# A sparse four-layer graph network on one core: the second half's tail is advanced ahead of the first, and query and input steps are emitted ahead of tail steps

## The chip, the cores and the metric

The kernel runs on one core of a Trainium2 chip. The core has five engines that run side by side, each through its own stream of instructions in the order in which they were emitted: PE (matrix multiplication, with its weight loads shown apart as PEld), DVE (elementwise work and reductions), ACT (activations and copies out of PSUM), POOL (here: the issue of gathers, and small elementwise operations) and SP (issue of plain DMAs). The metric is the time of the device in microseconds (us), lower is better.

## What is computed

The input `x` holds 16 graphs' features, 16 x 1024 x 128 in float32, and `adj` one 1024 x 1024 adjacency matrix with about 8 edges a row that all graphs share. Four layers follow one another. Layers 0, 2 and 3 are attention over the neighbours with a feed-forward block:

```python
Q, K, V = h @ Wq, h @ Wk, h @ Wv                    # 8 heads of 16
scores = where(adj == 0, -inf, Q K^T / 4)
x = h + (softmax(scores) V) @ Wo + bo
x = layer_norm(x)                                   # gain, shift
x = layer_norm(x + relu(x @ W1 + b1) @ W2 + b2)
```

Layer 1 is a graph attention with one head, whose scores are leaky sums of two terms per edge, followed by a residual and one layer norm; it has no feed-forward block.

## The kernel before

**Units and parts.** Since the graph is sparse, keys and values of every node lie in a DRAM table, and the kernel gathers the rows of each node's neighbours. Work is cut into units: layer, group of eight graphs (two groups), tile of 128 nodes (eight tiles), 64 units in all. A unit's edges are cut into parts. In an attention layer tile 0 has seven parts and every other tile five; the last part of a unit ("MIX") is half as large as the others. Part by part, DVE multiplies gathered keys by the queries (`products`, L868), reduces to scores (`exponentials`, L891), ACT takes the exponential (L895), DVE multiplies gathered values by it (`weighted`, L919), and PE sums the products by node (`summed`, L935, tile `acc`). POOL issues the gathers for the part four ahead (`gathered`, L856).

**Tails.** When a unit's sums are done, `divided` has DVE divide them, in two halves of four graphs each, into two tiles `o`, and starts one tail for each half. A tail is a Python generator: each `yield` ends a step. The steps of `attention_tail` are, in order:

- s0: PE transposes `o` (L596), ACT copies the result (`oT`, L598) and adds the bias to `x` (L640)
- s1: PE multiplies by `Wo` and by `centre` (L644, L645)
- s2: ACT squares with a running sum (L580); s3: POOL raises to the power -1/2 (L586); s4: ACT scales (`z`, L589)
- s5: PE transposes `z` (L596), ACT writes `x1` (L600)
- s6: PE multiplies by `W1` (L655), ACT takes the relu (`f1`, L659)
- s7: PE multiplies by `W2` and `centre` (L664, L668)
- s8, s9, s10: squares, power and scale again
- s11: PE transposes `z`, ACT writes `xT`; s12 and s13: PE multiplies by the next layer's `Wkv` (L538), ACT copies (L542); s14: SP writes the table. In the last layer s12 is a second transpose and copy (`outs`), and s13 POOL's scattered write of the output (L625).

The second half's tail begins with one empty step, so it is one step behind. `advance` gives every tail in the list one step.

**What sets the order.** The order is written out by hand: the main loop over parts emits, for each part, products, the sums of two parts before, `others()`, exponentials, `others()`, the weighted products of the part before and a gather, `others()`. I call these three calls slots 1, 2 and 3 of a part. Each call advances the tails at a pace that spreads 16 steps over a unit (about one per slot), and then takes one step of something else: `queries` of the next unit, or else `loaded` (in layer 0, the input of the unit after next), or else a step that projects the other group's input (`slow`, layer 0's first group only). Counting the five-part unit's parts from zero, the queries' four steps come in slots 2 and 3 of part 1 and slots 1 and 2 of part 2: PE multiplies by `Wq` (L819) and ACT copies `q` (L823), then four matmuls spread the rows over partitions (L828) into four PSUM tiles and ACT copies them into `qr` (L831); then the same for the second half. The tails of the unit before take their steps from slot 3 of part 1 on:

| slot | first half | second half | other step |
|---|---|---|---|
| part 1, 3 | s0 | (empty) | queries: spread, first half |
| part 2, 1 | s1 | s0 | queries: Wq, second half |
| part 2, 2 | s2 | s1 | queries: spread, second half |
| part 2, 3 | s3 | s2 | (queries end) |
| part 3, 1 | s4 | s3 | layer 0: POOL issues the gather of the first half's `rows` (L784) |
| part 3, 2 | s5 | s4 | |
| part 3, 3 | s6 | s5 | layer 0: PE transposes `rows`, ACT copies; POOL issues the second half's |
| part 4, 1 | s7 | s6 | |
| part 4, 2 | s8 | s7 | layer 0: the second half's `rows` are transposed |
| part 4, 3 | s9 | s8 | |
| next unit, part 0, slots 1, 2, 3 | s10, s11, s12 | s9, s10, s11 | |
| next unit, part 1, slot 1 | s13 | s12 | |
| next unit, part 1, slot 2 (two steps of the tails) | s14 | s13, s14 | queries: Wq, first half |

**Buffers.** `bank` hands out PSUM tiles from a pool of four; a transpose, a `W1` product or one spread matmul takes one of them each, and it is free again when ACT has copied it. The tails' sums have two PSUM tiles of their own (`yps`). `f1` is single, `oT`/`x1` and `z` are double.

Of the kernel before, what the change touches and what calls it, by code (L numbers as in the profile page):

```python
# [12 lines left out]
F32 = mybir.dt.float32  # L13
# [7 lines left out]
P = 128  # L21
D = 128
H = 8
HD = 16
FF = 256
F = FF // P
# [17 lines left out]
G = B // GR  # L44
HF = 2
GH = G // HF
# [4 lines left out]
J = P // 32  # L51
# [37 lines left out]
MOST = max(sum(map(len, _pieces)) for _pieces in PIECES)  # L89
# [33 lines left out]
def sparse_path(ctx: ExitStack, tc: tile.TileContext, a: dict, out: bass.AP, flag):  # L123
# [9 lines left out]
    def bank(shape):  # L133
        return banks.tile(shape, F32, tag="ps", name="ps")
# [39 lines left out]
    reps = ctx.enter_context(tc.tile_pool(name="reps", bufs=2))  # L174
    ones_ = ctx.enter_context(tc.tile_pool(name="ones_", bufs=1))
    twos = ctx.enter_context(tc.tile_pool(name="twos", bufs=2))
    exps = ctx.enter_context(tc.tile_pool(name="exps", bufs=2))
    scratch = ctx.enter_context(ExitStack())
    s1 = scratch.enter_context(tc.tile_pool(name="s1", bufs=1))
# [425 lines left out]
    def finish(l, g, t, h, z, gain, shift):  # L605
# [22 lines left out]
            in_=o.rearrange("p g d -> p (g d)"), in_offset=None,  # L628
        )

    def attention_tail(l, g, t, h, o):
        layer = LAYERS[l][0]
        p = {n: w[layer, n] for n in ATTN if (layer, n) in w}
        xt = xs[l, g, t][:, h]
        for _ in range(h):
            yield
        oT = twos.tile([P, GH, P], F32, tag="oT", name="oT")
        turned(o, oT)

        nc.scalar.activation(xt, xt, AF.Identity, bias=p["bo"])  # L640
        yield
        ps = ybanks.tile([P, GH, D], F32, tag="yps", name="yps")
        for i in range(GH):
            nc.tensor.matmul(ps[:, i, :], oT[:, i, :], p["Wo"], start=True, stop=False)  # L644
            nc.tensor.matmul(ps[:, i, :], xt[:, i, :], centre, start=False, stop=True)  # L645
        yield
        z = yield from normed(ps)
        yield
        x1 = twos.tile([P, GH, P], F32, tag="oT", name="x1")
        turned(z, x1, p["ln1_g"], p["ln1_b"])  # L650
        yield
        f1 = ones_.tile([P, F, GH * P], F32, tag="f1", name="f1")
        for f in range(F):
            ps = bank([P, GH * P])
            nc.tensor.matmul(  # L655
                ps, p["W1"][:, f * P : (f + 1) * P], x1.rearrange("p g n -> p (g n)"),
                start=True, stop=True,
            )
            nc.scalar.activation(f1[:, f, :], ps, AF.Relu, bias=p["b1"][:, f : f + 1])  # L659
        yield  # L660
        ps = ybanks.tile([P, GH, D], F32, tag="yps", name="yps")
        for i in range(GH):
            for f in range(F):
                nc.tensor.matmul(  # L664
                    ps[:, i, :], f1[:, f, i * P : (i + 1) * P], p["W2"][:, f, :],
                    start=(f == 0), stop=False,
                )
            nc.tensor.matmul(ps[:, i, :], x1[:, i, :], centre, start=False, stop=True)  # L668
        yield
        z = yield from normed(ps)  # L670
        yield
        yield from finish(l, g, t, h, z, p["ln2_g"], p["ln2_b"])
# [55 lines left out]
    def at_once(g):  # L728

        spare = reps.tile([P, J, ROW], F32, tag="qr", name="spare")  # L730

        def fetch(t):
            if t < T:
                nc.sync.dma_start(
                    spare[:, t % J, :], a["x"][t * P : (t + 1) * P, columns(g, 0, HF)]
                )

        for t in range(3):
            fetch(t)
        yield  # L740
        for t in range(T):
            fetch(t + 3)
            rows = spare[:, t % J, :].rearrange("p (h g d) -> p h g d", h=HF, g=GH)
            both = []
            for h in range(HF):
                kv = None
                if h:
                    kv = exponents()[:, : 2 * GH * D].rearrange("p (c g d) -> p c g d", c=2, g=GH)
                both.append(natural(g, t, h, rows[:, h], kv))
            while both:  # L750
                advance(both)
                yield

    def exponents():
        return exps.tile([P, max(MOST, 2 * D // HD) * G * H], F32, tag="ex", name="ex")


    units = [(l, g, t) for l in range(len(LAYERS)) for g in range(GR) for t in range(T)]
# [8 lines left out]
    es, prs, exs, qs, qx, ofs, accums = {}, {}, {}, {}, {}, {}, {}  # L767

    def is_attention(u):
        return LAYERS[units[u][0]][1] is ATTN  # L770
# [28 lines left out]
    def queries(u):  # L799

        l, g, t = units[u]
        if not is_attention(u):
            ps = bank([P, J + 1, G])
            for j in range(J):
                nc.tensor.matmul(ps[:, j, :], rep_of(j, True), srcs[g, t], start=True, stop=True)
            for k, j in enumerate(SHARED[t]):
                at = slice(64 * k, 64 * k + 64)
                nc.tensor.matmul(
                    ps[at, MIX, :], rep_of(j, True)[:, at], srcs[g, t], start=True, stop=True
                )  # L810
            ofs[u] = smalls.tile([P, J + 1, G], F32, tag="of", name="of")
            nc.scalar.copy(ofs[u], ps)
            return
        qs[u] = reps.tile([P, J, ROW], F32, tag="qr", name="qr")
        for h in range(HF):
            q = ones_.tile([P, GH * D], F32, tag="q", name="q")
            ps = bank([P, GH, D])
            for i in range(GH):
                nc.tensor.matmul(  # L819
                    ps[:, i, :], xs[l, g, t][:, h, i, :], w[LAYERS[l][0], "Wq"],  # L820
                    start=True, stop=True,
                )
            nc.scalar.copy(q, ps.rearrange("p g d -> p (g d)"))  # L823
            yield
            pss = []
            for j in range(J):
                ps = bank([P, GH * D])
                nc.tensor.matmul(ps, rep_of(j), q[32 * j : 32 * j + 32], start=True, stop=True)  # L828
                pss.append(ps)
            for j in range(J):  # L830
                nc.scalar.copy(qs[u][:, j, h * GH * D : (h + 1) * GH * D], pss[j])  # L831
            yield
# [49 lines left out]
    def exponentials(i):  # L882
        u, pieces = parts[i]
        t = units[u][2]
        heads = H if is_attention(u) else 1
        sc = smalls.tile([P, es[i].shape[1], G * heads], F32, tag="sc", name="sc")
        if u not in exs:
            exs[u] = exponents()[:, : MOST * G * heads].rearrange("p (c a) -> p c a", a=G * heads)
        ex, n = exs_of(i)
        if is_attention(u):  # L890
            nc.vector.tensor_reduce(  # L891
                sc[:, :n, :], prs[i][0][:, :n, :].rearrange("p k (a d) -> p k a d", d=HD),
                mybir.AxisListType.X, ALU.add,
            )
            nc.scalar.activation(ex, sc[:, :n, :], AF.Exp, scale=1.0 / HD**0.5)  # L895
        else:
            k = 0
            for piece in pieces:
                m = k + len(piece)
                nc.vector.tensor_tensor(  # L900
                    sc[:, k:m, :], es[i][:, k:m, ROW:], of_piece(ofs[u], piece), ALU.add
                )
                k = m
            nc.vector.scalar_tensor_tensor(
                sc[:, :n, :], sc[:, :n, :], SLOPE, sc[:, :n, :], ALU.mult, ALU.max
            )
            nc.scalar.activation(ex, sc[:, :n, :], AF.Exp)
# [55 lines left out]
    def divided(u):  # L963

        l, g, t = units[u]
        heads, d = (H, HD) if is_attention(u) else (1, D)
        den = bank([P, G * heads])
        for n, c in enumerate(sum(PIECES[t], [])):
            marked(t, c, den, exs[u][:, n, :])
        both = smalls.tile([P, 2, G * heads], F32, tag="both", name="both")  # L970
        yield
        nc.vector.reciprocal(both[:, 1, :], den)
        for h in range(HF):
# [14 lines left out]
    tails = []  # L988
# [2 lines left out]
    slow = []  # L991

    def advance(gens):
        for gen in list(gens):
            if next(gen, "end") == "end":
                gens.remove(gen)

    pace = [0.0, 0.0]

    def idle():  # L1000
        return slow if held[0] or not busy[0] else []

    def others():
        pace[0] += pace[1]
        while pace[0] >= 1.0:
            advance(tails)
            pace[0] -= 1.0
        for gens in (fronts or loads or idle(),):
            if not gens:
                continue  # L1010
            got = next(gens[0], "end")
            if got == "end":
                gens.pop(0)
            if got == "idle":
                advance(idle())

    with tc.manual_schedule():
        wide = [gather_buffer() for _ in range(EDGES)]
# [27 lines left out]
        smalls = ctx.enter_context(tc.tile_pool(name="smalls", bufs=3))  # L1046
# [8 lines left out]
        for i in range(len(parts) + 2):  # L1055
            here = i < len(parts)
            u = parts[i][0] if here else len(units)
# [58 lines left out]
            advance(tails)  # L1116


    fine = smalls.tile([P, 2, G * H], F32, tag="both", name="fine")
    nc.vector.tensor_scalar(fine, seen, LIMIT, None, ALU.is_lt)  # L1120
    counts = const.tile([P, 3], F32, name="counts")
    nc.vector.tensor_reduce(counts[:, 0:1], fine, mybir.AxisListType.XY, ALU.min)
# [428 lines left out]
```

## Time and profile before

| | |
|---|---|
| three runs | 2548.26, 2549.46 and 2554.35 us, median 2549.46 |
| the profiled execution's own time | 2562.74 us |
| span in its profile | 2561.0 us, mean granted PE clock 0.911 |
| busy, share of the span | PE 82%, DVE 75%, ACT 58%, POOL 57%, PEld 51% |
| DMA | 636 MB, 248 GB/s over the span |

How to read it: each engine's busy time is its instructions' own; a wait is idle time of an engine ahead of an instruction, put down to what ended it. PE's matmuls are pipelined and their ends modelled. In a line of the timeline the columns are start and length in us, the engine, the line of the kernel, the operation, output and input by name, the shapes, how many instructions were merged, and in brackets the idle time before and what released it. The stages, read from which lines run: up to about 200 us the graph is sorted and the first table is built; layer 0 runs until about 860 us, layer 1 until about 1200, layer 2 until about 1890, layer 3 to the end. A unit of an attention layer takes some 38 to 42 us, a unit of layer 1 some 20.

### The profile page before, as it was taken

What the parts mean: (1) busy time and instruction counts of PE and PEld (TensorE: products, weight loads), DVE (VectorE), ACT (ScalarE), POOL (GpSimd) and SP (SyncE); (2) the same over time, 40 slices, a digit from 0 to 9 for tenths busy, and PEclk for the clock granted to TensorE, in tenths of its full rate; (3) what the DMA queues carried; (4) which work ended last, traced back from release to release, by engine and by line L of the source; (5) the groups of instructions that cost most, each with busy time, mean ns of one, the idle gap of its engine ahead of it and who ended that gap; (6) DMA issues with size and microseconds to landing.
All of it is one profiled execution on the core that took longest, in us unless ns stands there. A gap on an engine that the chain in (4) does not pass through costs nothing. (4 is left out here: it accounts for less than half of the span.)

```text
span 2561.0 us, 36646 instructions
## 1 busy us (share of the span) xinstructions
PE 2102.6 (82%) x13124; PEld 1303.1 (51%) x13124; DVE 1930.3 (75%) x1470; ACT 1474.6 (58%) x4640; POOL 1450.8 (57%) x978
## 2 busy tenths in 40 slices
PE   6558989788887888988788888988888787888786
PEld 5425656445554554554455554555555454445454
DVE  7887787587877466667887879788797877787782
ACT  3216776565665444455476656667666665566555
POOL 3334666366666588784545545455555656665652
PEclk8679999899898999999899999999999898989888
DMA  7646888667678589898777877788777667567660
GB/s 251 232 170 230 293 280 287 210 227 252 231 257 260 175 282 327 281 322 297 276 256 248 298 258 261 255 283 277 264 267 254 222 240 260 203 222 257 222 222 24
DMA packets 168461, 636.05 MB, mean 248 GB/s; under 512 B 38328, under 2 KB 41144, under 8 KB 119774
## 3 DMA queue, kind: packets, MB, share of 16 engines
q0 software_dynamic: 92672, 485.09, 54.2%
q1 hardware_dynamic: 75600, 148.55, 17.4%
q8 instruction: 105, 1.72, 0.3%
q14 instruction: 84, 0.69, 0.1%
HBM read 603.11 MB, written 92.34 MB: 272 GB/s over the span
## 5 line engine op out<-in xcount | busy, mean ns | idle before, releaser
L856 POOL DMA_INDIRECT e<-table,idx x600 | 925.7, 1543 | 455.9 <-DVE pr L919 245.6
L919 DVE TENSOR_TENSOR pr<-e,ex 128x2048 f32<-128x2048 f32 (+1 forms) x336 | 689.5, 2060 | 205.0 <-ACT ex L895 174.2
L868 DVE TENSOR_TENSOR pr<-e,qr 128x2048 f32<-128x2048 f32 x204 | 460.7, 2258 | 177.8 <-PE acc L935 80.7
L586 POOL TENSOR_TENSOR rstd<-total,power 128x4 f32<-128x4 f32 x224 | 333.1, 1490 | 392.6 <-ACT z L580 385.4
L935 PE MATMUL acc<-pr,marks 128*32 128x512 f32 x2656 | 495.1, 618 | 38.2 <-DVE pr L919 38.2
L891 DVE TENSOR_REDUCE sc<-pr 128x128 f32<-128x2048 f32 (+1 forms) x252 | 518.5, 2058 | 8.6
L580 ACT ACTIVATE z<-yps,root 128x128 f32<-128x128 f32 x896 | 318.5, 378 | 98.5 <-PE yps L683 49.8
L596 PE MATMUL ps<-ident,z 128*128 128x128 f32 x896 | 212.7, 338 | 161.8 <-ACT z L589 161.7
L589 ACT ACTIVATE z<-yps,rstd 128x128 f32<-128x128 f32 x896 | 257.3, 381 | 102.4 <-POOL rstd L586 102.3
L596 PEld LDWEIGHTS ps<-ident,z 128*128 128x128 f32 x896 | 136.0, 159 | 345.4 <-ACT z L589 251.8
L659 ACT ACTIVATE f<-ps,b 128x512 f32<-128x512 f32 x192 | 131.9, 690 | 275.8 <-PE ps L655 275.8
L655 PE MATMUL ps<-x,W 128*128 128x512 f32 x384 | 249.1, 783 | 35.9 <-ACT x L600 35.8
L664 PE MATMUL yps<-W,f 128*128 128x128 f32 x1536 | 259.7, 287 | 17.0 <-ACT f L659 15.9
L664 PEld LDWEIGHTS yps<-W,f 128*128 128x128 f32 x1536 | 212.2, 196 | 77.5 <-ACT f L659 58.6
L935 PEld LDWEIGHTS acc<-pr,marks 128*32 128x32 f32 x2656 | 102.0, 112 | 283.8 <-issue 223.9
L538 PE MATMUL ps<-Wkv,xT 128*128 128x256 f32 x768 | 208.7, 416 | 32.7 <-ACT xT L600 24.1
L831 ACT COPY qr<-ps 128x512 f32<-128x512 f32 x384 | 197.0, 600 | 61.3 <-PE ps L828 55.7
L580 ACT ACTIVATION_READ_ACCUMULATOR z<-yps,root 128x1 f32 x896 | 194.1, 217 | 0.0
L542 ACT COPY kv<-ps 128x512 f32<-128x512 f32 x176 | 103.3, 589 | 140.9 <-PE ps L538 117.1
L538 PEld LDWEIGHTS ps<-Wkv,xT 128*128 128x128 f32 x768 | 146.4, 202 | 73.1 <-ACT xT L600 30.0
L644 PE MATMUL yps<-Wo,oT 128*128 128x128 f32 x768 | 160.9, 292 | 6.0 <-ACT oT L598 6.0
L645 PE MATMUL yps<-centre,x 128*128 128x128 f32 x768 | 158.0, 288 | 6.6
(159 smaller groups left out, 2663.6 us busy)
## 6 DMA issues: line engine op xcount, KB each, us to landing
table<-kv SPq DMA_DIRECT2D x88, 512.0 KB
qx<-qr SPq DMA_DIRECT2D x96, 256.0 KB
kept<-xT SPq DMA_DIRECT2D x96, 256.0 KB
x<-kept SPq DMA_DIRECT2D x48, 512.0 KB
e<-table,idx POOLq DMA_INDIRECT x600
table<-kv SPq DMA_DIRECT2D x32, 256.0 KB
edges<-in_adj SPq DMA_DIRECT2D x8, 512.0 KB
spare<-in_x SPq DMA_DIRECT2D x8, 512.0 KB
```

Source lines behind the costliest of these rows:

```text
L538: nc.tensor.matmul(ps[:, k, :], x[:, i + k, :], w[LAYERS[l][0], "Wkv"], start=True, stop=True,)
L580: nc.scalar.activation(z[:, i, :], y[:, i, :], AF.Square, scale=D**-0.5, bias=root, accum_out=total[:, i : i + 1],)
L586: nc.gpsimd.tensor_tensor(rstd, total, power, ALU.pow)
L589: nc.scalar.activation(z[:, i, :], y[:, i, :], AF.Copy, scale=rstd[:, i : i + 1])
L596: nc.tensor.transpose(ps[:, i, :], z[:, i, :], ident)
L655: nc.tensor.matmul(ps, p["W1"][:, f * P : (f + 1) * P], x1.rearrange("p g n -> p (g n)"), start=True, stop=True,)
L664: nc.tensor.matmul(ps[:, i, :], f1[:, f, i * P : (i + 1) * P], p["W2"][:, f, :], start=(f == 0), stop=False,)
L856: nc.gpsimd.indirect_dma_start(out=es[i][:, k, :], out_offset=None, in_=tables[l, g][:, :], in_offset=bass.IndirectOffsetOnAxis(ap=idx[:, ...
L868: nc.vector.tensor_tensor(prs[i][0][:, :n, :], es[i][:, :n, :ROW], qx[u].rearrange("p (o c) -> p o c", o=1) if (MIX, 0) in piece else of_p ...
L891: nc.vector.tensor_reduce(sc[:, :n, :], prs[i][0][:, :n, :].rearrange("p k (a d) -> p k a d", d=HD), mybir.AxisListType.X, ALU.add,)
L919: nc.vector.tensor_tensor(prs[i][k0 // 2][:, :m, :].rearrange("p k (a d) -> p k a d", d=d), es[i][:, k0 : k0 + m, base : base + ROW].rearr ...
L935: nc.tensor.matmul(outs[32 * j : 32 * j + 32], marks[:, mark, :], rhss, start=(r == 0 and chunk[0] != MIX), stop=(chunk == last),)
```

## The change

`advance` walks its list backwards, so in each slot the second half takes its step before the first half does. In `others()` the other step (queries, inputs, other group) is emitted before the tails' steps. Since the second half now writes its `f1` before the first half has emitted the reads of its own, `f1` gets a pool of two buffers, `fs`. To pay for the space, the exponentials' tiles are cut to what the parts need, the half of the first projection that borrowed one of them borrows an `f1` buffer instead, and three small tiles (`sc`, `of`, `both`) move from a pool of three buffers to one of two. The core of the diff (a few lines of context and the same move of `of`, `both` and `fine` are left out):

```diff
+    fs = ctx.enter_context(tc.tile_pool(name="fs", bufs=2))
...
+    def hidden():
+        return fs.tile([P, F, GH * P], F32, tag="f1", name="f1")
...
-        f1 = ones_.tile([P, F, GH * P], F32, tag="f1", name="f1")
+        f1 = hidden()
...
                 if h:
-                    kv = exponents()[:, : 2 * GH * D].rearrange("p (c g d) -> p c g d", c=2, g=GH)
+                    kv = hidden().rearrange("p f (a d) -> p f a d", d=D)
...
     def exponents():
-        return exps.tile([P, max(MOST, 2 * D // HD) * G * H], F32, tag="ex", name="ex")
+        return exps.tile([P, MOST * G * H], F32, tag="ex", name="ex")
...
-        sc = smalls.tile([P, es[i].shape[1], G * heads], F32, tag="sc", name="sc")
+        sc = exps.tile([P, es[i].shape[1], G * heads], F32, tag="sc", name="sc")
...
     def advance(gens):
-        for gen in list(gens):
+        for gen in reversed(gens):
             if next(gen, "end") == "end":
                 gens.remove(gen)
...
     def others():
-        pace[0] += pace[1]
-        while pace[0] >= 1.0:
-            advance(tails)
-            pace[0] -= 1.0
         for gens in (fronts or loads or idle(),):
             if not gens:
                 continue
...
             if got == "idle":
                 advance(idle())
+        pace[0] += pace[1]
+        while pace[0] >= 1.0:
+            advance(tails)
+            pace[0] -= 1.0
```

More of the change, by code (lines that the diff above doesn't have):

```diff
@@ L810, in queries @@
                 )
-            ofs[u] = smalls.tile([P, J + 1, G], F32, tag="of", name="of")
+            ofs[u] = exps.tile([P, J + 1, G], F32, tag="of", name="of")
             nc.scalar.copy(ofs[u], ps)
@@ L969, in divided @@
             marked(t, c, den, exs[u][:, n, :])
-        both = smalls.tile([P, 2, G * heads], F32, tag="both", name="both")
+        both = exps.tile([P, 2, G * heads], F32, tag="both", name="both")
         yield
@@ L1116, in sparse_path @@
             advance(tails)
-    fine = smalls.tile([P, 2, G * H], F32, tag="both", name="fine")
+    fine = exps.tile([P, 2, G * H], F32, tag="both", name="fine")
     nc.vector.tensor_scalar(fine, seen, LIMIT, None, ALU.is_lt)
```

## The prediction

> **What bounds the kernel now.** I read the page's shares first (PE 82%, DVE 75%: no engine full), then the windows of 100 us (layers 0, 2 and 3 mostly at 80 to 90% on PE, layer 1 with 85 to 87% of the DMA engines' time taken), then the waits, and last the timeline of one regular unit, 1700 to 1738 us. In the waits of layers 2 and 3 (1240 to 2500 us), DVE's first lines are
>
> ```profile
> DVE pr L919 <- ACT ex L895: 93.7, 33, 6.9
> DVE pr L868 <- PE acc L935: 47.4, 16, 3.3
> ```
>
> so DVE waits for ACT and for PE. The unit's timeline says which of them sets the pace:
>
> ```profile
> 1703.19 1.73 PE L828 MATMUL ps<-q,rep 32*128 32x512 f32 x8 [0.24 <-ACT q L823]
> ...
> 1715.31 1.10 PE L596 MATMUL ps<-ident,z 128*128 128x128 f32 x4 [1.94 <-ACT z L589]
> ...
> 1717.29 1.27 PE L655 MATMUL ps<-x,W 128*128 128x512 f32 x2 [0.87 <-ACT x L600]
> ...
> 1724.96 0.69 ACT L659 ACTIVATE f<-ps,b 128x512 f32<-128x512 f32 x1 [3.03 <-PE ps L655]
> ...
> 1726.56 0.49 PE L664 MATMUL yps<-W,f 128*128 128x128 f32 x2 [0.37 <-ACT f L659]
> ...
> 1726.68 1.23 DVE L919 TENSOR_TENSOR pr<-e,ex 128x1024 f32<-128x1024 f32 x1 [2.29 <-ACT ex L895]
> ...
> 1731.17 2.29 DVE L868 TENSOR_TENSOR pr<-e,qr 128x2048 f32<-128x2048 f32 x1 [3.26 <-PE acc L935]
> ...
> 1733.11 1.13 PE L538 MATMUL ps<-Wkv,xT 128*128 128x256 f32 x4 [0.87 <-ACT xT L600]
> ```
>
> The reader is to see that PE has only 4.3 us of idle in 38 (0.24, 1.94, 0.87, 0.37, 0.87), all of it waiting for ACT in the tail, while DVE, once its 2.29 us for the exponential are over, waits 3.26 us more for PE's sums. PE, with ACT's tail behind it, is the loop that closes; DVE has slack. The 2.29 us are the visible target: exponential and relu stand in one ACT queue, the relu waited 3.03 us for the second half's `W1`, and that stood on PE behind the first half's `W2`. In layer 0 PE also waits for inputs:
>
> ```profile
> 343.85 1.86 POOL L784 DMA_INDIRECT rows<-in_x,places  x1 [0.30 <-issue]
> ...
> 352.27 0.63 PE L596 MATMUL ps<-ident,rows 128*128 128x128 f32 x4 [1.54 <-DMA rows<-in_x,places]
> ```
>
> Issued at 343.85, landed at 352.27: 8.4 us, though PE did `W2` of both halves in between.
>
> **What the Trainium skill says.** "TensorE: Matmul & The Clock Gate", section "What's actually happening": PE's clock falls to half after an idle window of about 3.4 us. The trace agrees: after the two waits around the first norm's transposes `W1` of the first half takes 3.57 us up to the next instruction in most units, 1.82 where PE had not waited (1551, 1875, 2501 us). Same page, "Architectural detail": ACT's and DVE's queues are strictly first in, first out, PE pulls only weight loads ahead. The relu and exponential above agree. So order of emission is order of execution, and a waiting instruction holds all behind it.
>
> **The change part by part.** Times are those of the unit at 1700 us; I re-time it by hand, with each instruction's length from its row.
>
> *Queries ahead.* In part 1, slot 2, `Wq` (0.9) now precedes the second half's last `Wkv` (0.9), which covers the copy of `q` (0.59): the 0.24 wait goes. In slot 3 the four spread matmuls (1.1 together) precede the transposes of `o` (0.45). The spread takes all four PSUM tiles; two are free only after ACT's copies at 1703.1 and 1703.2, so it ends at 1704.35, and the transposes follow at once. But ACT now copies `qr` four times (2.05) before `oT` and the bias (1.3): `Wo` of the first half waits for them until about 1706.85. `Wo` of the second half then ends at 1711.56 against 1711.45: nothing gained, 0.1 lost. Where `o` is late (layer 3, 1.19 us of wait in most units) the spread fills that wait, some 0.2 to 1 us.
>
> *First norm, second half ahead.* The squares of the first half come after the copies now, so its power ends at 1714.45 instead of 1713.9; ACT is through with both squares by 1714.5, and the scaling starts at 1714.55 instead of 1714.84. Then comes the second half's scaling, which waits for its power (1715.8) and takes 1.14, and `x1` of the first half stands behind it (0.78): `W1` begins at 1717.9 instead of 1717.29, 0.6 late. The second half's transposes (0.85 up to the next instruction) now lie before it, inside the wait: net 0.25 gained.
>
> *Feed-forward.* PE runs W1, W1, W2, W2 instead of W1, W2, W1, W2. The relus no longer wait behind `W2`, the stall of 0.37 (0.45 with its ramp) goes, and the exponential is done about 1.8 us earlier. DVE's 2.29 us go; next late is PE's sum, so they become more of the 3.26 us wait and are priced at nothing.
>
> *Second norm.* By the same step, the second half's scaling precedes the first half's `xT`, whose `Wkv` starts at 1734.0 instead of 1733.11; the transposes drawn ahead return 0.53: 0.36 lost.
>
> Sum for a unit of layers 2 and 3: 0.1 - 0.25 - 0.45 + 0.36, about -0.25; with late `o` -0.5. Some 30 units: **-11 us**.
>
> *Inputs ahead (layer 0).* 14 units load inputs. In part 4, slot 2, the second half's `rows` are now transposed before the second half's `W2` (3.0) instead of after it. Their gather on POOL stays behind the same two gathers of keys, so it lands when it did. Twelve of the issues I followed were transposed 6.6 to 9.5 us after issue, and those that made PE wait landed at 7.1 to 8.6; PE now comes 3.2 us sooner. Taking a landing of 7.5 (6.8 in the second group), added waits are 0.7 to 3.2 us, about 28 in all, and `W2`, the sums and DVE's wait for them are behind. In part 3, slot 1, POOL issues the first half's `rows` (1.0) ahead of the second half's power, which by the step above holds up `x1`; and `rows` (landing 3.5 to 4.7 us after issue) are needed before `W1` instead of after: 1 us in each of the six units without filler work, 6. The norms and feed-forward give back 0.4 a unit, 6. Layer 0: **+28 us**.
>
> *Nothing.* Layer 1 waits for gathers (5 to 7 us a unit for DMA), and its tail has no feed-forward: 0, between -5 and +5. Two buffers for `sc`: DVE's weighted product of the same part already waits for the exponential that frees it, before the next but one reduction; if that cover failed, 0.32 us a part, 80 us in all, at most; it can't fail by order on DVE. `of` and `both` are free a unit earlier. SP's transfers keep their order among themselves, and so do POOL's gathers of keys and output writes. Setup: the eight projections that borrow another buffer still have two; reversed order of four generators in unit 0: -5 to +5. I take 0 for each.
>
> Sum: +28 - 11 = +17 us, against the profiled execution's 2562.74, which stands 13 above the median; carried over, 2549.5 + 17 = **2566**.
>
> **The rivals.** About 0.3%, 7.6 us, is what a measurement of this kernel can tell from no change.
>
> *Slower, my forecast* (chance 0.50): as above; own range 2557 to 2595, with rows' cost full or half and the norms at 0 to +0.5 a unit.
>
> *Faster, by PE's clock* (0.36). Place: the first norm. Today PE does one group of transposes (1.1) in 3.9 us between the sums' end and `W1`; after, both groups in 4.5. If that keeps PE awake, `W1` takes 1.82 instead of 3.57: 1.75 us in each of some 40 units, 70 us. It decides from 17 / 1.75, ten units on, and gives 2566 - 70 = 2496 at the full, 2531 at the half. For it: a unit at 614 us ran `W1` at 1.82 after the same waits. Against: the idle total is no smaller, and the longer stretch can as well catch a window more often. The same side is reached if the inputs land sooner because POOL is freer, up to 28 us.
>
> *The same* (0.14): the second half's rows cost half (14), the rest as computed: 2549.5 + 14 + 6 - 6 - 11 = 2552.5. The change does what it says here only in order: every gain is taken back at the next wait.
>
> The range, 2515 to 2595, reaches into the faster case to half of its clock gain and into the slower one to rows at their full price.
>
> **What would show it.** Right: in layers 2 and 3 the half-size weighted product no longer waits for the exponential, and DVE's wait for `acc` grows; ACT's wait of the relu (275.8 us) falls by over 100; W1's `x1` wait stays near or above zero with `W1` still 3.5 us long; in layer 0 PE's wait for `rows` (33.1 us) doubles or more, and layer 0 ends some 20 to 30 us later while layers 2 and 3 are 5 to 15 shorter. Wrong: `W1` at 1.8 us in many units, `rows` not waited for, or DVE's saved 2.29 us showing as shorter units.

## The result and the profile after

The changed kernel takes 2619.02 us (median of four runs, 2614.11 to 2633.86) beside 2549.27 for the kernel before on the same chip: ratio 1.0279, 95% interval 1.0235 to 1.0323, some 70 us slower. The profiled execution of the changed kernel is one of 2614.11 us, span 2612.3, mean granted PE clock 0.897.

Line numbers behind the new pool are one higher, and those behind `hidden` four: the products L868 are now L872, the sums L935 are L939, the relu L659 is L663, the transposes L596 are L597.

The first view is again DVE's waits over layers 2 and 3 (columns: us in total, times, longest), now of 1295 to 2550 us:

```profile
DVE pr L872 <- PE acc L939: 62.9, 15, 5.1
DVE pr L872 <- DMA e<-table,idx: 57.9, 33, 5.9
DVE pr L923 <- ACT ex L899: 38.7, 26, 3.7
```

The wait for the exponential fell from 93.7 to 38.7 us and that for the sums rose from 47.4 to 62.9; part of it went to the gathers instead, which stood at 41.5 us in this view of the kernel before. The unit that answers to the one of before, at 1752 to 1792 us:

```profile
1768.15 1.10 PE L597 MATMUL ps<-ident,z 128*128 128x128 f32 x4 [1.35 <-ACT z L590]
...
1771.26 1.25 PE L597 MATMUL ps<-ident,z 128*128 128x128 f32 x4 [2.01 <-ACT z L590]
...
1772.70 4.91 PE L659 MATMUL ps<-x,W 128*128 128x512 f32 x8 [0.20 <-ACT x L601]
...
1774.82 0.69 ACT L663 ACTIVATE f<-ps,b 128x512 f32<-128x512 f32 x1 [1.49 <-PE ps L659]
...
1777.45 0.61 PE L668 MATMUL yps<-W,f 128*128 128x128 f32 x4
...
1778.97 1.22 DVE L923 TENSOR_TENSOR pr<-e,ex 128x1024 f32<-128x1024 f32 x1
...
1784.86 2.29 DVE L872 TENSOR_TENSOR pr<-e,qr 128x2048 f32<-128x2048 f32 x1 [4.68 <-PE acc L939]
```

Eight `W1` stand together, the relu waits 1.49 us, `W2` and the half-size product don't wait, and DVE waits 4.68 us for the sums instead. That is the predicted picture, and the unit is not shorter for it: 38.8 us against 38.0, measured from one of DVE's reciprocals to the next; a reciprocal closes a unit.

So where did 70 us go? I cut the traces at those reciprocals (unit 0 to 63; units 0 to 7 are layer 0's first group). "Buffers only" is the experiment below with the old order and the new buffers:

| us | before | buffers only | after |
|---|---|---|---|
| start to end of unit 1 | 239.2 | 244.8 | 255.8 |
| **end of unit 1 to 6 (layer 0, first group)** | **207.6** | **207.4** | **259.8** |
| unit 6 to 8 | 109.1 | 111.4 | 107.6 |
| unit 8 to 15 (layer 0, second group) | 291.9 | 289.9 | 292.7 |
| unit 15 to 31 (layer 1) | 352.7 | 340.3 | 340.4 |
| unit 31 to 47 (layer 2) | 656.0 | 651.7 | 657.7 |
| unit 47 to 63 (layer 3) | 664.7 | 667.3 | 657.4 |

The loss is in one place: 52 us in the five units from 1 to 6, which grew from 41.5 to 52 us each, and 11 to 17 ahead of them. These are the units in which the other group's projection (`at_leisure`) runs as filler. The 12 us by which layer 1 is shorter are not the order's: the old order with the new buffers takes 340.3 as well.

The windows of that stretch (columns: us, busy time and instructions of PE, PEld, DVE, ACT and POOL, PE's clock, DMA share, GB/s), before and then after:

```profile
239.20:446.80 207.60, 184.21 (x1258) 125.78 (x1257) 161.84 (x91) 149.43 (x480) 128.54 (x80) 0.98 0.84 285
```

```profile
255.80:515.60 259.80, 201.60 (x1261) 139.74 (x1262) 163.58 (x90) 150.40 (x483) 106.23 (x80) 0.90 0.67 230
```

The same work, and every engine and the DMA less full. PE's 17 us more of busy time go with a clock of 0.90 instead of 0.98; the rest is waiting. The waits in it, of the changed kernel:

```profile
DVE pr L872 <- PE acc L939: 61.2, 9, 12.8
ACT kv L560 <- DMA table<-kv: 35.8, 6, 7.7
...
PE ps L597 <- DMA rows<-in_x,places: 26.8, 10, 4.7
```

Before, they were 16.1 us for `acc`, none for the table and, for the rows:

```profile
PE ps L596 <- DMA rows<-in_x,places: 6.5, 5, 1.9
```

There are two new waits, then: PE for `rows`, which was predicted, and ACT for a table write, which was not. The timeline shows both in one unit:

```profile
315.81 0.37 ACT L560 COPY kv<-ps 128x256 f32<-128x256 f32 x1 [6.67 <-DMA table<-kv]
...
316.37 0.71 PE L559 MATMUL ps<-wg,xT 128*128 128x130 f32 x4 [3.60 <-ACT src L568]
...
337.77 0.98 POOL L788 DMA_INDIRECT rows<-in_x,places  x1 [0.30 <-issue]
...
341.93 0.61 PE L668 MATMUL yps<-W,f 128*128 128x128 f32 x4
...
346.68 1.12 PE L597 MATMUL ps<-ident,rows 128*128 128x128 f32 x4 [3.92 <-DMA rows<-in_x,places]
347.59 1.06 PE L668 MATMUL yps<-W,f 128*128 128x128 f32 x4
...
354.34 2.29 DVE L872 TENSOR_TENSOR pr<-e,qr 128x2048 f32<-128x2048 f32 x1 [12.12 <-PE acc L939]
```

The projection of the other group and that of the tails share a pair of `kv` buffers. The projection's last table write (512 KB) is issued on SP at 306.15; a tail's first copy into that buffer is next in ACT's queue at 309.1, so ACT stands until 315.8 with the copies of `q`, `both` and `qr` behind it, and PE with it. Later PE has done half of `W2` when it comes to the second half's rows, issued at 337.77 and there at 346.7, 8.9 us later. After the 3.92 us of idle, four `W2` matmuls take 1.06 us instead of 0.61. The Trainium skill's "TensorE: Matmul & The Clock Gate", "What's actually happening", has PE fall to half speed after an idle window of about 3.4 us; the lines agree. The sums come late by all of it, and DVE waits 12.12 us.

The write also takes longer than it did. Before, it was issued at 317.02, and the tail's copy took its buffer at 322.55, 5.5 us later, without a wait for it. The DMA queues in the first 3.5 us behind the issue show what it met (q1 carries SP's plain transfers, q0 POOL's gathers; columns: packets, MB, share of the 16 engines). Before (317.0 to 320.5), SP's queue had the engines almost alone and moved more than the 512 KB of the write:

```profile
q1 hardware_dynamic: 416, 0.79, 58.0%
q0 software_dynamic: 1, 0.01, 1.8%
```

After (306.1 to 309.6), the write fell among the gathers:

```profile
q0 software_dynamic: 111, 0.62, 75.3%
q1 hardware_dynamic: 42, 0.09, 6.3%
```

It is so in all five units of the stretch: 0.01 to 0.16 MB of gathers in those 3.5 us before, 0.51 to 0.75 MB after.

### The profile page after: what moved, and what is told of

It is laid out like the page before. It is cut to its first block, busy times and chain, and to the rows that moved or that the text cites. A ratio compares the mean times of both kernels' runs of the same rounds, so it can differ in the third digit from the quotient of the medians.

```text
span 2612.3 us, 36726 instructions
## 1 busy us (share of the span) xinstructions
PE 2149.9 (82%) x13124; PEld 1315.5 (50%) x13124; DVE 1935.0 (74%) x1470; ACT 1469.3 (56%) x4640; POOL 1406.3 (54%) x978
## 5 line engine op out<-in xcount | busy, mean ns | idle before, releaser
L872 DVE TENSOR_TENSOR pr<-e,qr 128x2048 f32<-128x2048 f32 x204 | 461.7, 2263 | 235.6 <-PE acc L939 137.6
L939 PE MATMUL acc<-pr,marks 128*32 128x512 f32 x2656 | 499.3, 619 | 40.4 <-DVE pr L923 40.4
L587 POOL TENSOR_TENSOR rstd<-total,power 128x4 f32<-128x4 f32 x224 | 283.7, 1269 | 441.8 <-ACT z L581 432.6
L597 PE MATMUL ps<-ident,z 128*128 128x128 f32 x896 | 237.4, 355 | 174.4 <-ACT z L590 170.3
L597 PEld LDWEIGHTS ps<-ident,z 128*128 128x128 f32 x896 | 130.9, 151 | 349.5 <-ACT z L590 277.8
L659 PE MATMUL ps<-x,W 128*128 128x512 f32 x384 | 250.0, 797 | 7.9 <-ACT x L601 7.9
L939 PEld LDWEIGHTS acc<-pr,marks 128*32 128x32 f32 x2656 | 102.6, 112 | 293.4 <-issue 216.2
L668 PE MATMUL yps<-W,f 128*128 128x128 f32 x1536 | 240.4, 280 | 0.0
L663 ACT ACTIVATE f<-ps,b 128x512 f32<-128x512 f32 x192 | 132.0, 687 | 154.6 <-PE ps L659 153.7
L832 PE MATMUL ps<-q,rep 32*128 32x512 f32 x768 | 146.1, 681 | 27.0 <-ACT q L827 26.4
```

The costliest lines, as they stand in the source:

```text
L587: nc.gpsimd.tensor_tensor(rstd, total, power, ALU.pow)
L597: nc.tensor.transpose(ps[:, i, :], z[:, i, :], ident)
L659: nc.tensor.matmul(ps, p["W1"][:, f * P : (f + 1) * P], x1.rearrange("p g n -> p (g n)"), start=True, stop=True,)
L668: nc.tensor.matmul(ps[:, i, :], f1[:, f, i * P : (i + 1) * P], p["W2"][:, f, :], start=(f == 0), stop=False,)
L872: nc.vector.tensor_tensor(prs[i][0][:, :n, :], es[i][:, :n, :ROW], qx[u].rearrange("p (o c) -> p o c", o=1) if (MIX, 0) in piece else of_p ...
L939: nc.tensor.matmul(outs[32 * j : 32 * j + 32], marks[:, mark, :], rhss, start=(r == 0 and chunk[0] != MIX), stop=(chunk == last),)
```

## The experiments

Two theories at first. **A**: the loss comes from what is emitted ahead of the tails in layer 0's first group, by the shared buffer (A1) or by the order on the engines, rows first (A2). **B**: it comes from the second half going first. Ratios are to the kernel before on the same chip, with 95% intervals; "stretch" is the end of unit 1 to that of unit 6. It is read from one profile of each run. Lines added by an edit shift the line numbers in its views by up to twelve. The expectations call PE TensorE and ACT ScalarE.

**Old order, second half first.**

```diff
     def others():
+        pace[0] += pace[1]
+        while pace[0] >= 1.0:
+            advance(tails)
+            pace[0] -= 1.0
         for gens in (fronts or loads or idle(),):
...
-        pace[0] += pace[1]
-        while pace[0] >= 1.0:
-            advance(tails)
-            pace[0] -= 1.0
```

> The second half still goes first and has a hidden tile of its own, but the tails are emitted first again in every slot, ahead of queries, inputs and the other group's projection. Theory A (the loss of about 68 us lies in layer 0's first group and comes from what is emitted ahead of the tails there): 2545 to 2560 us, units 1 to 6 back at 40 to 44 us each. Theory B (the second half going first makes the loss): 2605 to 2620 us, those units stay at 50 to 56 us.

2557.35 us, 1.0065 (1.0040 to 1.0091); stretch 218.5. A holds for most of the loss, but not all: the second half's lead alone costs 0.65%, and it brings a wait of its own in the stretch:

```profile
ACT kv L560 <- DMA table<-kv: 22.8, 5, 6.0
```

**Queries alone ahead.**

```diff
     def others():
-        for gens in (fronts or loads or idle(),):
...
+        ahead = bool(fronts)
+        if ahead and next(fronts[0], "end") == "end":
+            fronts.pop(0)
         pace[0] += pace[1]
         while pace[0] >= 1.0:
             advance(tails)
             pace[0] -= 1.0
+        if ahead:
+            return
+        got = "idle"
+        if loads:
+            got = next(loads[0], "end")
+            if got == "end":
+                loads.pop(0)
+        if got == "idle":
+            advance(idle())
```

> Only the queries (and the other generators of the same list) are emitted ahead of the tails; rows and the other group's projection come behind them again; second half first. Theory A with rows or projection as the culprit: 2535 to 2555 us, first group as before the change, layers 1 and 3 some 10 us shorter each as they are after it. If the queries ahead are the culprit, or theory B: 2605 to 2620 us.

2571.39 us, 1.0118 (1.0071 to 1.0165); stretch 222.3. Above what A gave for it, well below B. The interval overlaps that of the old order, so a cost of the queries ahead isn't shown; a gain isn't either.

**Everything behind the tails while the other group's projection runs.**

```diff
+        def step():
+            gens = fronts or loads or idle()
...
+        behind = bool(slow)
+        if not behind:
+            step()
         pace[0] += pace[1]
...
+        if behind:
+            step()
```

> As after the change, but while steps of the other group's projection remain (layer 0's first group) everything is emitted behind the tails, as before the change. Theory A: 2540 to 2555 us, the first group as before, all later units as after the change. Theory B: 2605 to 2620 us. It differs from the run with the old order everywhere only after unit 7, so the two together give what the new order is worth there: by the profiles 10 to 25 us less, if it is that order; nothing, if the second half's lead alone makes it.

2562.84 us, 1.0089 (1.0058 to 1.0119); stretch 217.2. The expected place, but 8 us over the expected time. It does no better than the old order everywhere: behind unit 7 the new order of queries and inputs is worth nothing that shows.

**A buffer of its own for the projection's keys and values.**

```diff
-            if kv is None:
-                kv = twos.tile([P, 2, GH, D], F32, tag="kv", name="kv")
+            if kv is None and not l:
+                kv = ones_.tile([P, 2, GH, D], F32, tag="kv", name="kv")
             for i in range(0, GH, 2):
+                if l:
+                    kv = twos.tile([P, GH * D + GH], F32, tag="kvg", name="kv")
...
-        kv = twos.tile([P, GH * D + GH], F32, tag="kv", name="kv")
+        kv = twos.tile([P, GH * D + GH], F32, tag="kvg", name="kv")
         if h == 0:
```

> As after the change, but the projection of the other group has its own buffer for keys and values, so that no tail of layer 0 waits for its table write (41.9 us of ScalarE waits in 7 times, first group). In return one buffer in the setup instead of two, up to 15 us later at unit 0, and the tails of layers 1 and 2 write their tables in halves. Theory A1 (that buffer makes the loss): units 1 to 6 at 43 to 48 us, 35 to 45 us back over them. Theory A2 (the order on the engines makes it, and the buffer's wait only fills idle time): under 10 us back over units 1 to 6.

Stretch 229.2, 30.6 us less than after the change: short of A1's 35 to 45, but with 45.8 us a unit inside its 43 to 48, and far from A2's. ACT's wait for the table is gone there, PE's for rows is 18.2 us. The whole is 2744.25 us, 1.0813 (1.0769 to 1.0858): the halved buffers in the tails of layers 1 and 2 did there what the shared pair did in the first group (layer 1 takes 384.9 us, layer 2 756.4). In the whole run:

```profile
ACT kv L546 <- DMA table<-kv: 261.1, 58, 9.6
```

A miss as a kernel. As a measurement it shows that ACT waiting for a table write is no filled idle time.

**First half first, the rest as changed.**

```diff
-        for gen in reversed(gens):
+        for gen in list(gens):
```

> As after the change, but the first half goes first again; queries, inputs and projection stay ahead of the tails. If the two parts of the change simply add (the run with the old order everywhere but the second half first lost 13 us in units 0 to 6 and 0.65% in all): 1.018 to 1.024 of the kernel before, 10 to 15 us less than after the change, units 1 to 6 at 48 to 52 us. If the second half's lead is what makes the fillers dear (theory B): 1.00 to 1.01, units 1 to 6 at 41 to 44 us.

2602.39 us, 1.0202 (1.0148 to 1.0256); stretch 248.4. The two parts add, within the intervals: 2.0% for the steps emitted ahead, 0.65% for the second half's lead, 2.8% for both. B falls.

**The projection alone behind.**

```diff
-        for gens in (fronts or loads or idle(),):
...
+        got = None
+        gens = fronts or loads
+        if gens:
+            got = next(gens[0], "end")
...
+        else:
+            got = "idle"
         pace[0] += pace[1]
...
+        if got == "idle":
+            advance(idle())
```

> As after the change, but the steps of the other group's projection come behind the tails; queries and input rows stay ahead, second half first. Queries alone ahead left units 0 to 6 25 us later than before the change, all three ahead 69 us. Theory rows (TensorE waits for rows ahead of the tails): 20 to 35 us come on top of those 25, units 1 to 6 at 47 to 51 us, PE's wait for rows 25 to 30 us in the first group. Theory projection (its steps ahead make the rest): units 1 to 6 at 43 to 46 us, the whole within 10 us of the run with queries alone ahead.

Stretch 240.4, 48.1 us a unit, as the rows theory has it, with both waits still there (17.4 us for the rows, below that theory's 25 to 30, and 32.7 for the table write); but the whole, 2578.01 us and 1.0109 (1.0056 to 1.0162), lies on that of queries alone, as the other theory has it. The run doesn't decide.

**Rows' transposes one step later.**

```diff
                 yield "idle"
                 yield "idle"
+                yield "idle"
                 turned(rows, xs[units[u]][:, h])
```

> As after the change, with one more idle step between the fetch of the rows and their transposes, so that they land before TensorE comes to them (it waited 28 us for rows in the first group). Theory rows: 25 to 40 us back, PE's wait for rows in the first group under 5 us, units 1 to 6 at 45 to 48 us. Theory buffer alone (the tails' wait for the other group's table write is the loss and the wait for rows fills idle time): under 8 us back.

2545.94 us, 0.9996 (0.9970 to 1.0022); stretch 219.5. One line takes back as much as the whole loss, twice what the rows theory expected. Part of that is a gain elsewhere: the units 6 to 8 take 95.2 us, 14 less than before the change, and the last run returns to them. In the stretch:

```profile
DVE pr L873 <- PE acc L940: 27.4, 4, 6.8
...
PEld ps L597 <- DMA rows<-in_x,places: 2.5, 3, 0.8
```

ACT's wait for the table write is not in the list at all: the added "idle" steps also move the projection forward, so that its last table write is issued 6.3 to 7.6 us ahead of the tails' first copies instead of mostly 2.5. This run took away two things at once, and the next two separate them.

**The same, without the added step of the projection.**

```diff
                 yield "idle"
                 yield "idle"
+                yield
                 turned(rows, xs[units[u]][:, h])
```

> Again one more step between the fetch of the rows and their transposes, but one in which the other group's projection does not advance, so that its table write stays in the last slots of a unit, just ahead of the layer-1 projection of the tails that needs the same pair of buffers. Measured from the end of unit 1 to that of unit 6 (before the change 208 us, after it 260, with the late rows 220): rows theory 220 to 230 us and no wait for rows; the theory that the late rows helped only by moving the table write ahead of the tails: 245 us or more, with ScalarE's wait for the table write still 25 us or more.

2563.68 us, 1.0083 (1.0058 to 1.0109); stretch 229.6. No wait for rows, and ACT's wait as large as ever:

```profile
ACT kv L560 <- DMA table<-kv: 35.1, 5, 8.5
```

**Order of the change, rows not waited for.** (This kernel leaves out the use of the fetched rows, so its layer 0 doesn't compute on the inputs.)

```diff
                 yield "idle"
                 yield "idle"
+                if u:
+                    rows = ident.rearrange("p (o n) -> p o n", o=1).to_broadcast([P, GH, P])
                 turned(rows, xs[units[u]][:, h])
```

> Everything in the order of the changed kernel, and the rows of layer 0 are still fetched, but the transposes ahead of the tails read the identity in place of the rows, so that they never wait for the fetch (the layer's inputs x are then not the rows). Rows theory (TensorE standing at those transposes is the loss, and the wait for the table write follows from the bunching): 215 to 232 us from the end of unit 1 to that of unit 6, the whole 30 us or more below the changed kernel. Buffer theory (the wait for the other group's table write is a loss of its own, from the emission order): 240 to 252 us, ScalarE's wait for the table write as large as before, 30 us or more.

2552.69 us, 1.0043 (1.0029 to 1.0057); stretch 225.7, which is the rows theory's number, with the buffer theory's wait:

```profile
ACT kv L560 <- DMA table<-kv: 34.8, 6, 7.5
DVE pr L874 <- DMA e<-table,idx: 28.7, 5, 6.5
...
DVE pr L874 <- PE acc L941: 11.9, 4, 3.3
```

DVE's largest wait here is for the gathers (3.1 us in the late rows), so what this run still loses is not the table write's alone.

With the four runs 40 of the 52 us are accounted for: they come with the two waits and go with them. Stretch, in us:

| | PE waits for rows | it doesn't |
|---|---|---|
| ACT waits for the table write | 259.8 (changed kernel) | 225.7, 229.6 |
| it doesn't | 229.2 (own buffer) | 219.5 (late rows) |

Either wait by itself costs 6 to 10 us here; the second on top of it costs 30 to 34. The first three runs above, each with an order of its own, belong in the upper right cell too, with 18.6 to 22.8 us of waiting for the table write and about 2 for rows; they take 217.2 to 222.3, about as long as with neither wait. Put against the sum of the two waits, 2.5, 18, 35 and 63 us of waiting give 219.5, 229.2, 225.7 to 229.6 and 259.8. The projection alone behind, with 50 us, lies near that line (240.4); the forward order, with 41.5 and 248.4, lies above it, so the sum alone doesn't set the time. That the first wait is taken up by slack in the units and the second is not is how I read these numbers; no run shows the slack itself.

The other 12 us stay when both waits are gone (219.5 against 207.6). PE's idle time in the stretch is then back to 22.4 us (23.4 before the change, 58.2 after it), but PE is busy for 13 us more than before, at a clock of 0.95 instead of 0.98. Why is not shown.

**Buffers only.**

```diff
-        for gen in reversed(gens):
+        for gen in list(gens):
...
     def others():
+        pace[0] += pace[1]
+        while pace[0] >= 1.0:
+            advance(tails)
+            pace[0] -= 1.0
         for gens in (fronts or loads or idle(),):
...
-        pace[0] += pace[1]
-        while pace[0] >= 1.0:
-            advance(tails)
-            pace[0] -= 1.0
```

> Only the buffers of the change: a hidden tile for each half and the small tiles moved; both orders as before. All theories: within 0.3% of the kernel before, 2532 to 2547 us where that takes 2539. It also gives a second profile of the old order: if layers 1 and 3 come out as long as in the profile before, the 11 and 16 us that the changed kernel gained there are real; if they come out 10 us shorter each, that was the one execution of before.

2550.81 us, 0.9993 (0.9974 to 1.0011). The moved tiles cost nothing in the whole, as predicted. This run is not the old kernel, though, and of the two gains that the changed kernel seemed to have, layer 1's goes with the buffers: the two kernels with the old ones take 352.7 and 349.1 us there (before, and the last run), the eleven profiles with the new ones, the own-buffer run aside, 339.0 to 344.4, whatever the order. Which of the tiles does it was not tried. Layer 3's gain goes with the second half's lead (667.3 here, 657.4 after): 661.4 to 667.3 us in the four profiles without it, 654.2 to 661.9 in nine with it. Layer 2 goes the other way, 649.2 to 656.0 against 653.9 to 666.2.

**Old order in the first group, changed order behind it, late rows.**

```diff
-        for gen in reversed(gens):
+        for gen in list(gens) if slow else reversed(gens):
...
                 yield "idle"
                 yield "idle"
+                yield "idle"
...
+        behind = bool(slow)
+        if not behind:
+            step()
...
```

> A version made from the findings: while steps of the other group's projection remain (layer 0's first group) tails first and first half first, as before the change; from there on the changed order, with the rows' transposes one idle step later. If the gains of the changed order behind the first group are real (by the profiles some 10 to 20 us against the old order): 0.990 to 0.996 of the kernel before. If they were only that one execution of before: 0.998 to 1.002.

2526.20 us, 0.9938 (0.9922 to 0.9955): faster than both kernels. But its profile is ahead of "buffers only" by 16 us between units 6 and 8 (95.0 against 111.4), and its layers 2 and 3 (660.9 and 657.2) sum to within 1 us of those of "buffers only". So the last run asks whether the order has any part in it.

**The kernel before with late rows and nothing else.**

```diff
                 yield "idle"
                 yield "idle"
+                yield "idle"
                 turned(rows, xs[units[u]][:, h])
```

> The kernel before, with nothing but one more idle step between the fetch of layer 0's rows and their transposes. The run with both orders was 0.62% faster than the kernel before, and against the run with the buffers alone its profile is 16 us shorter between units 6 and 8 and near it elsewhere: the added idle steps let the other group's projection advance more often, so that less of it is left when the second group's gathers need it. If that is where the 0.62% comes from: 0.992 to 0.996, 95 to 100 us from the end of unit 6 to that of unit 8 (before 109), nothing elsewhere. If it comes from the changed order behind the first group: 0.998 to 1.003.

2540.36 us, 0.9958 (0.9939 to 0.9978). Between units 6 and 8, groups of `Wkv` (instructions | busy, mean ns | idle before), before and then this run:

```profile
L538 PE MATMUL ps<-Wkv,xT 128*128 128x256 f32 x16 | 4.0, 392 | 2.0 <-ACT xT L598 2.0
```

```profile
L538 PE MATMUL ps<-Wkv,xT 128*128 128x256 f32 x8 | 2.0, 392 | 1.3 <-ACT xT L598 1.3
```

Half as much of the projection is left there, and these two units take 96.4 us instead of 109.1, of which the units 1 to 6 give back 6.5 (214.1). That less is left is not the whole of it: in the changed kernel it is half as much too, and they take 107.6. Of the 12.7 us, 5.2 lie in the second of the two units (50.1 before, 44.9 here), and it is as short (45.7) in the late rows without the added step, where as much of the projection is left as before; the other 7.5 lie in the first (59.0 and 51.5), which that run doesn't shorten (59.2). Most of the gain of the version above is the added idle step. What its order adds is not shown: the intervals overlap.

## Why the prediction was wrong

The direction held, the size did not: +70 us against +17, and 2619 us is above the range of 2515 to 2595. Layer 0 ends 62 to 68 us later, where +28 was put.

- **Inputs ahead (layer 0), +28: this step failed.** The size of the wait was about right: PE's wait for `rows` rose from 33.1 to 76.0 us, 43 against the 34 that the step added. What failed is the price. It took each us of wait as one us of time and gave the units with filler work nothing beyond it. In the second group 21.0 us of wait were there (before 3.6), and the group is 1 to 3 us longer than the old order's; the three runs of the changed order that don't wait for rows are 3.0, 5.6 and 11.8 us shorter than the changed one. In the first group the stretch cost 52 us: 40 because the wait for rows met another, 12 without a cause that is shown.
- **Nothing, "SP's transfers keep their order among themselves": the missing term.** Around this write they do. What counts is how soon after it a tail needs its buffer, what else the DMA engines move meanwhile, and what stands behind the copy that waits. Before, the buffer was needed 5.5 us after the issue and was free. In the changed kernel ACT came to it 3.0 us after the issue, and it was free after 9.7 (306.15 to 315.81). Over all waits for it in the stretch, in all runs, the time from issue to release was 6.1 to 11.2 us. No run moves the gathers alone, so how much of the wait is theirs and how much the earlier need is not shown. The Trainium skill's "DMA: Bandwidth & Descriptors", "Anatomy of one DMA — SWDGE (gpsimd) path", gives about 2.0 us and 436 GB/s for a transfer by itself on the GpSimd path, an estimate of 3.2 us for 512 KB; these transfers, issued from SP beside the gathers, took two to three and a half times that. The second half's lead was never looked at for its effect on this pair of buffers: alone, it brought 22.8 us of this wait.
- **Queries ahead, first norm, feed-forward, second norm: -11 us.** The waits moved as stated: the relu's from 275.8 to 153.7 us, `W1`'s for `x1` from 35.8 to 7.9, DVE's for the exponential into its wait for `acc` (80.7 to 137.6 over the run). Layer 3 became 7 to 10 us shorter, where -0.5 a unit made 8. Layer 2 was to become 4 shorter and is 2 to 6 longer, without a cause that I can show. Both together became 4 to 6 us shorter here; over all profiles (the own-buffer run aside) they take 1313 to 1321 us with the first half ahead and 1309 to 1323 with the second, so the -11 is not shown. Layer 1, put at 0, became 9 to 12 us shorter in the kernels with the new buffers.
- **The rivals.** The faster one fell at its own test: `W1` takes 797 ns in the mean, 783 before, so the clock didn't return; it was lost in the first group instead, 0.98 to 0.90. The reading under this rival was loose: the waits ahead of `W1` in the unit shown are 1.94 and 0.87 us, each shorter than the window of 3.4 us put beside them, and after the same waits `W1` took 1.82 us at 614 us and 3.57 at 657. The same-time one fell with the price of the rows.

## What to carry to other kernels

When a step is moved ahead in an in-order queue, price two distances and not only its length: from the issue of the transfer that it consumes to the step, and from the transfer that empties a buffer to the next writer of that buffer, with all that stands behind the writer. Ask too what else the DMA will be moving then: the same write that freed its buffer within 5.5 us took 9.7 among gathers. Price the stalls of one loop together: here each alone cost at most 10 us and both 40. A consumer of a transfer that is moved forward needs its issue moved too, or one more step in between. And profile the parts of a change apart before a difference of 10 us in a stage is put down to one of them: layer 1's came with the buffers, not with the order.

## What was not expected of the hardware

A table write of 512 KB held its buffer for 5.5 us at most where the gathers had nearly paused, and for 6.1 to 11.2 us from issue to release in the waits that came up while they ran. Halving the writes and the buffers in the tails of two layers brought 58 such waits, up to 9.6 us each.
